# A history-attention recommender on one core: 1600 steps written out without a loop, and the head behind them reordered

## The chip, the core and the metric

One core of one Trainium2 chip runs the kernel. TensorE (PE) multiplies matrices into PSUM, VectorE (DVE) and ScalarE (ACT) work elementwise, GpSimd (POOL) issues the gathers of table rows, SyncE (SP) issues most other DMAs. The metric is the device time of one execution in microseconds (us): the median of 3 runs before the change is 32,292.97 (32,289.11 to 32,293.9).

## What is computed

The batch has 16,384 examples, each with 200 history items. With embeddings `h` (history), `it` (item), `u` (user) and `c` (category), 64 numbers each, the reference is, cut to what matters:

```python
def dice(x, alpha, axis):
    mean = jnp.mean(x, axis=axis, keepdims=True)
    var = jnp.var(x, axis=axis, keepdims=True)
    p = jax.nn.sigmoid((x - mean) * jax.lax.rsqrt(var + EPS))
    return x * (p + alpha * (1.0 - p))

h = i_emb[hist]                                  # 200 x 16384 x 64
feat = concatenate([h, itb, h - itb, h * itb])   # itb: it for every line
a = dice(feat @ au_W1 + au_b1, au_alpha, axis=1) # statistics over the batch, per history line
w = a @ au_W2 + au_b2
cur = sum(w * h, axis=0)
z = concatenate([u, it, c, cur], axis=-1)        # 256 numbers
z = dice(z @ W1 + b1, alpha1, axis=0)            # first layer, 80 numbers
z = dice(z @ W2 + b2, alpha2, axis=0)            # second layer, 40 numbers
return z @ W3 + b3                               # last layer, 2 numbers
```

All numbers are 32-bit floats. Each `dice` needs a mean and a variance over the whole batch before any of its outputs can be made.

## The kernel before

**Tiling.** The batch is cut into 8 chunks of 2,048 examples. A *step* `k` handles one chunk of one history line, so there are 200 x 8 = 1,600 steps. A chunk is gathered by 16 gathers of 128 rows each (`fetch`, L346, through `gather`, L127) into one of 16 buffers `rows`. Chunks 5 and 6 of some history lines have one of their 16 pieces fetched row by row by SP or ScalarE instead (the classes `SyncQueue` and `ScalarQueue`; `ask` in L447 hands out these fetches, the loads of their addresses and their scaling ahead of time). There are 25,350 history gathers in all.

**A step** (L421) works on several chunks at once: it fetches chunk `k`, transposes chunk `k-1` (`turn`), multiplies it with the attention weights (`product`), adds the item's part and takes statistics of chunk `k-3` (`hidden`, `measure`), and weighs and sums chunk `k-10` (`gate`, `weights`, `weigh`, where LAG is 10) into the running sums `cur`. After the last chunk of a line, `moments` turns its statistics into a scale and a shift. The order on each engine is, but for small shifts, the order in which the program is written.

**The loop.** `BODY` is 192 history lines. A loop over them (L504) has two passes of 96 lines, 768 steps each, written out inside. The other 8 lines, 64 steps, are written out behind it. In the first steps of the first pass, the chunks `k-1`, `k-3` and `k-10` do not exist yet; the same code runs on zeroed buffers then. For this, the start zeroes `hT`, `xs`, `hm` and `rows[2:]`, prepares statistics and clears PSUM.

**The start** (L465 to L501). SP loads ids, first history ids and attention weights. GpSimd gathers the 8 item chunks into `rows[0]` and `rows[1]` in turn. VectorE transposes each (`transpose`, four 64x512 instructions), SP stores it to DRAM for later reloads (`load_items`), and TensorE and ScalarE make the item's part `itp`. A gather that overwrites a buffer waits for the transposes of what was there. Behind the items come first fetches of single rows, `head_weights` (L229: VectorE zeroes the head's weight tiles, SP issues 45 small loads into them, VectorE computes `1 - alpha` and the averaging matrices `same_a` and `same_b`) and the zeroing of `rows[2:]` (L501).

**The head** (from L508). For each chunk `c`, 16 gathers fetch category rows (`j = 2c`) and 16 user rows (`j = 2c + 1`). `head_layer` multiplies four 128x1024 tiles (user, item, category, `cur`; `cur` is transposed first) with `w1a` and `w1b`: 64 of the 80 outputs of two half batches fill 128 rows of PSUM (`za`), the other 16 of each fill 32 rows, and four chunks of these are stacked to 128 rows (`zb`). Category and item are multiplied when the category rows are there, `cur` and user when the user rows are. `head_moments` (L555) gives mean and variance over the batch, with two small matmuls with `same_a` or `same_b` that average over rows. `dice` (L574) is one sigmoid on ScalarE and two VectorE operations (L577, L578). The second layer (L585 to L595) multiplies `cur` (which now holds the first 64 outputs) with `w2a`, 128 rows, and one 32-row quarter of `ab` with 32 rows of `w2b` (L592), into four PSUM tiles in turn; ScalarE evacuates (L594), VectorE takes statistics (L518). The last layer multiplies with `w3`, four chunks into one PSUM tile, and for each group of four, transposes, adds the bias and sends the outputs (L604 to L624).

Of the kernel before, what the change touches and what calls it, by code (L numbers as in the profile page):

```python
# [14 lines left out]
P = 128  # L15
# [5 lines left out]
LPB = 96  # L21
# [15 lines left out]
def din_kernel(  # L37
# [36 lines left out]
    BODY = L - L % LPB if L > LPB else 0  # L74
# [79 lines left out]
    def transpose(dst, of):  # L154
        for i in range(2):
            for e in range(2):
                nc.vector.transpose(by_tile(dst[ts(e, D)], i), of[ts(i, D), :, ts(e, S)])  # L157
# [58 lines left out]
    w2b = make("w2b", P, P)  # L216
# [4 lines left out]
    res = [make(f"res{i}", P, 4, TD, ZO) for i in range(2)]  # L221
# [7 lines left out]
    def head_weights():  # L229
# [8 lines left out]
        for g in range(2):  # L238
# [23 lines left out]
    class Queue:  # L262


        def __init__(self, engine, tiles, group, lead, span, buffers, addresses):
            self.engine, self.tiles, self.group, self.lead, self.span = engine, tiles, group, lead, span
            self.buffers, self.addresses, self.n = buffers, addresses, len(buffers)
            self.per = P // group

# [12 lines left out]
        def events(self, k, count):  # L282
            for m in range(count):
                q = m * self.per
                if self.when(q) - 8 == k:
                    yield self.load, m
                if self.when(q) - 5 == k:
                    yield self.scale, m
            for q in range(count * self.per):
                if self.when(q) == k:  # L290
                    yield self.fetch, q

        def load(self, m, l0):
            j = NC + SIDES.index(self.tiles[m % len(self.tiles)][1])
            nc.sync.dma_start(self.addresses[m % self.n], r_hist[ds(l0 + self.line(m), 1), j * P : (j + 1) * P])

        def scale(self, m, l0):
            nc.vector.tensor_scalar_mul(self.addresses[m % self.n], self.addresses[m % self.n], ROW)

        def fetch(self, q, l0):  # L300
# [120 lines left out]
    def step(k, last=None, rows_by_scalar=()):  # L421

        def has(j):
            return last is None or j <= last

        if has(k):
            fetch(k)
# [11 lines left out]
        for q, l0 in rows_by_scalar:  # L439
            by_scalar.fetch(q, l0)  # L440
# [6 lines left out]
    def ask(k, l0, n, more):  # L447
        late = []
        for q in queues:
            per = len(q.tiles)  # L450
            for what, m in q.events(k, n * per // PERIOD + (more and 2)):
                if q is by_scalar and what == q.fetch:
                    late.append((m, l0))
                else:
                    what(m, l0)
        return late

    def steps(l0, n, more):
        for k in range(n * ND):
            l, c = divmod(k, ND)  # L460
            if c == 0 and l + 1 < n + more:
                load_hist_ids((l + 1) % IDX, l0 + l + 1, by_address(l + 1))
            step(k, rows_by_scalar=ask(k, l0, n, more))

    with tc.manual_schedule():  # L465
# [6 lines left out]
        for t in (*hT, *xs, *side, *aside, *hm):  # L472
# [21 lines left out]
        for t in px:  # L494
            layer(t, [(blk_m, hm[0])])
        load_items(0)
        for k in range(-16, 0):
            ask(k, 0, L, 0)
        head_weights()
        for t in rows[2:]:  # L500
            nc.vector.memset(t, 0.0)  # L501
# [6 lines left out]
    K = (L - BODY) * ND  # L508
# [3 lines left out]
    zb = flat_rows[3:5]  # L512
    pz = [px[K % 2], px[(K + 1) % 2], pg, py]
# [141 lines left out]
```

## Time and profile before

| | us |
|---|---|
| median of 3 runs | 32,292.97 |
| the profiled execution | 32,292.57 |
| its span, first to last instruction | 32,290.8 |
| GpSimd busy | 24,281.4 (75%) |
| VectorE busy | 22,882.8 (71%) |
| TensorE busy | 9,918.7 (31%) |
| ScalarE busy | 6,057.9 (19%) |

The profile is of one execution. An instruction's row gives the source line, the engine, the operation, what it writes and reads, and how often; then the busy time, or start and duration. In brackets or behind a bar stands the idle time of the engine ahead of it and what ended that. Issuing a DMA is not busy time; a gather (`DMA_INDIRECT`) is GpSimd's own work. "PEclk" is the share of TensorE's clock that was granted. One 128x128x512 matmul in 32-bit floats shows as two matmul records.

The share of busy time is even over the run: of 40 equal slices, the first is 6 tenths for VectorE, the last 5, all others 7; GpSimd is at 7 in all but the last.

### The profile page before, as it was taken

The numbers are of one execution on the slowest core, as the hardware profiler recorded it, in microseconds if no ns is written. First come the engines' busy times: TensorE is split into PE (matmuls) and PEld (weight loads), VectorE is DVE, ScalarE is ACT, GpSimd is POOL, SyncE is SP. The second block draws the span as 40 slices with busy tenths as digits, with TensorE's granted clock in tenths as the row PEclk, the third lists the DMA queues.
The fourth block names the chain that finished last, engine by engine and source line by source line (L and its number), as shares of the span: only waits on it lengthen the run. The fifth ranks groups of instructions, "written<-read, shape, count | busy, mean of one in ns | idle before, by whom it ended". The sixth has DMA issues, their size and how long they took to land.

```text
span 32290.8 us, 175696 instructions
## 1 busy us (share of the span) xinstructions
PE 9918.7 (31%) x13212; PEld 3717.7 (12%) x13212; DVE 22882.8 (71%) x31911; ACT 6057.9 (19%) x5738; POOL 24281.4 (75%) x25739
## 2 busy tenths in 40 slices
PE   2333323333333333233233333333333333333334
PEld 1111111111111111111111111111111111111111
DVE  6777777777777777777677777777777777777775
ACT  1111111111111111111111111111111111111111
POOL 7777777777777777777777777777777777777776
PEclk6666666666666666666666666666666666666666
DMA  2222222222222222222222222222222222222221
GB/s 55 54 54 53 54 54 54 54 54 54 54 54 54 54 54 53 54 54 54 53 54 54 54 53 54 54 54 54 53 54 54 54 54 53 54 54 54 54 53 39
DMA packets 1179260, 1726.19 MB, mean 53 GB/s; under 512 B 559010, under 2 KB 559260, under 8 KB 1177980
## 3 DMA queue, kind: packets, MB, share of 16 engines
q0 software_dynamic: 823488, 844.90, 15.1%
q1 hardware_dynamic: 328604, 866.62, 7.8%
q14 instruction: 1175, 9.63, 0.1%
q10 hardware_dynamic: 25888, 3.33, 0.1%
q8 instruction: 105, 1.72, 0.0%
HBM read 1708.61 MB, written 4.33 MB: 53 GB/s over the span
## 4 chain that ended last, share of the span: by engine, by line
POOL 32%; issue 11%; DMA 4%; DVE 4%; ACT 1%; PE 0%; SPq 0%; DVEq 0%; POOLq 0%; ACTq 0%
POOL rows L128 32%; DMA rows<-in_L_rec_i_emb,idx 4%; DVE hT L157 1%; DVE xs L376 0%; DVE st L381 0%; DVE pg L359 0%; DVE py L358 0%; ACT L354 0%; DVE py L360 0%; DVE py L372 0%; ACT pg L354 0%; ACT pg L355 0%; DVE pg L364 0%; DVE other L408 0%; DVE mv L404 0%
## 5 line engine op out<-in xcount | busy, mean ns | idle before, releaser
L128 POOL DMA_INDIRECT rows<-in_L_rec_i_emb,idx x25350 | 23918.5, 944 | 7749.0 <-issue 7452.1
L162 PE MATMUL px<-hT,blk_h 128*128 128x512 f32 x6404 | 5972.1, 1088 | 21637.1 <-DVE xs L376 21622.7
L157 DVE STREAM_TRANSPOSE hT<-rows 64x512 f32<-64x512 f32 x6404 | 4518.4, 706 | 7674.6 <-DMA rows<-in_L_rec_i_emb,idx 7476.0
L391 ACT COPY py<-hT 128x1024 f32<-128x1024 f32 x1601 | 1627.3, 1016 | 24930.0 <-DVE hT L157 24930.0
L162 PEld LDWEIGHTS px<-hT,blk_h 128*128 128x128 f32 x6404 | 1880.6, 324 | 24758.2 <-DVE xs L376 23104.6
L162 PE MATMUL px<-hm,blk_m 128*128 128x512 f32 x6412 | 3970.5, 752 | 369.2 <-DVE hm L398 368.0
L358 DVE TENSOR_TENSOR py<-pg,xs 128x1024 f32<-128x1024 f32 x1610 | 1985.0, 1233 | 615.7 <-ACT pg L355 468.9
L162 PEld LDWEIGHTS px<-hm,blk_m 128*128 128x128 f32 x6412 | 1757.9, 277 | 3276.1 <-issue 1878.5
L381 DVE BATCH_NORM_STATS2 st<-xs 128x6 f32<-128x512 f32 x3206 | 2062.3, 685 | 55.1
L359 DVE STREAM_TRANSPOSE pg<-py 128x1024 f32<-128x1024 f32 x1610 | 2037.1, 1265 | 55.9
L360 DVE TENSOR_REDUCE py<-pg 128x32 f32<-128x1024 f32 x1610 | 1985.0, 1233 | 54.7
L372 DVE TENSOR_TENSOR py<-rows,pg 128x1024 f32<-128x1024 f32 x1610 | 1978.3, 1229 | 55.2
L373 DVE TENSOR_TENSOR cur<-py,cur 128x1024 f32<-128x1024 f32 x1610 | 1970.7, 1224 | 55.6
L376 DVE TENSOR_TENSOR xs<-px,itp 128x1024 f32<-128x1024 f32 x1603 | 1963.2, 1225 | 50.6
L354 ACT ACTIVATE pg<-xs,sh,rs 128x1024 f32<-128x1024 f32 x1610 | 1937.1, 1203 | 35.3 <-DVE py L372 32.6
L398 DVE TENSOR_TENSOR hm<-py,itT 128x1024 f32<-128x1024 f32 x1601 | 1933.9, 1208 | 0.0
L355 ACT ACTIVATE pg<-pg,au_al,au_1al 128x1024 f32<-128x1024 f32 x1610 | 1895.0, 1177 | 54.2
L364 DVE SCALAR_TENSOR_TENSOR pg<-py,au_bias,part 32x16 f32<-32x16 f32 x6440 | 1538.9, 239 | 227.0
L361 DVE COPY part<-py 64x32 f32<-64x32 f32 x1610 | 312.6, 194 | 55.9
L354 ACT ACT_TABLE_LOAD x204 | 261.7, 1283 | 3.6
L171 ACT ACT_TABLE_LOAD x203 | 260.4, 1283 | 7.5 <-PE pg L565 4.0
L408 DVE COPY other<-mv 32x2 f32<-32x2 f32 x804 | 158.6, 197 | 15.1
(138 smaller groups left out, 1514.0 us busy)
## 6 DMA issues: line engine op xcount, KB each, us to landing
itT<-items SPq DMA_DIRECT2D x1609, 512.0 KB
rows<-in_L_rec_i_emb,idx POOLq DMA_INDIRECT x25350
side<-in_L_rec_i_emb SPq DMA_DIRECT2D x19200, 0.2 KB
aside<-in_L_rec_i_emb ACTq DMA_DIRECT2D x12800, 0.2 KB
idx<-in_r_hist SPq DMA_DIRECT2D x200, 63.0 KB
items<-itT SPq DMA_DIRECT2D x8, 512.0 KB
idx<-in_r_hist SPq DMA_DIRECT2D x150, 0.5 KB
addr<-in_r_hist SPq DMA_DIRECT2D x150, 0.5 KB
```

Of the source, the lines that this page charges most:

```text
L128: nc.gpsimd.indirect_dma_start(out=dst[:, n, :], out_offset=None, in_=table, in_offset=bass.IndirectOffsetOnAxis(ap=ids, axis=0),)
L157: nc.vector.transpose(by_tile(dst[ts(e, D)], i), of[ts(i, D), :, ts(e, S)])
L162: nc.tensor.matmul(dst[:, ts(i, CH)], lhsT, rhs[:, ts(i, CH)], start=(first and j == 0), stop=(last and j == len(pairs) - 1), skip_group_c ...
L354: nc.scalar.activation(pg, xs[k % XR], AF.Sigmoid, bias=shifts[i], scale=rstds[i])
L358: nc.vector.tensor_mul(py, pg, xs[k % XR])
L359: nc.vector.transpose(pg, py)
L360: nc.vector.reduce_sum(total, pg.rearrange("p (n a) -> p n a", a=S), axis=mybir.AxisListType.X)
L372: nc.vector.tensor_mul(of, rows[k % ROWS], w.unsqueeze(2).to_broadcast([P, TD, D]))
L373: nc.vector.tensor_add(cur[k % ND], py, cur[k % ND])
L376: nc.vector.tensor_add(xs[k % XR], px[k % 2], itp[k % ND])
L381: nc.vector.bn_stats(stats[l % 3][:, 2 * c + i, :], xs[k % XR][:, ts(i, CH)])
L398: nc.vector.tensor_mul(hm[k % 2], py, itT[k % ITEMS])
```

## The change

The 1,600 steps are written out without a loop, `step` skips what does not exist at the start and the end, and what served the loop's first steps is gone (the zeroing of `hT`, `xs`, `hm` and `rows[2:]`, prepared statistics, cleared PSUM). `head_weights` moves ahead of the item gathers. In the head:

- `w2b` becomes four tiles of 128 rows, each zero outside one quarter, so that the second layer multiplies with 128 rows throughout.
- `cur` is transposed and multiplied with category and item, an iteration earlier than the user rows.
- The transposes of the last user chunk are split at its 12th piece.
- The two norms of the first layer share one chain; activation tables are loaded by small dummy activations (`table`).
- The first `dice` of each group of 32-row outputs comes behind the first of the 64-row outputs instead of ahead of all.
- In the last layer all eight `dice` come ahead of the transposes and outputs, and outputs alternate between SP's and ScalarE's queue. `res` lies in a row buffer that is free by then.

```diff
-LPB = 96
-    BODY = L - L % LPB if L > LPB else 0
...
-    def transpose(dst, of):
+    def transpose(dst, of, n0=0, n1=TD):
         for i in range(2):
             for e in range(2):
-                nc.vector.transpose(by_tile(dst[ts(e, D)], i), of[ts(i, D), :, ts(e, S)])
+                nc.vector.transpose(by_tile(dst[ts(e, D)], i)[:, n0:n1], of[ts(i, D), n0:n1, ts(e, S)])
...
-    w2b = make("w2b", P, P)
+    w2b = make("w2b", P, 4, P)
...
-                nc.sync.dma_start(w2b[r, g * ZA : g * ZA + Z2], W2[ZA:])
+                nc.sync.dma_start(w2b[r, j, g * ZA : g * ZA + Z2], W2[ZA:])
...
+    K = L * ND
-    def step(k, last=None, rows_by_scalar=()):
+    def step(k):
         def has(j):
-            return last is None or j <= last
+            return 0 <= j < K
+        rows_by_scalar = ask(k)
         if has(k):
+            l, c = divmod(k, ND)
+            if c == 0 and l + 1 < L:
+                load_hist_ids((l + 1) % IDX, l + 1, by_address(l + 1))
             fetch(k)
...
         attention_weights()
-        for t in (*hT, *xs, *side, *aside, *hm):
+        for t in (*side, *aside):
             nc.vector.memset(t, 0.0)
         for t in cur:
             nc.vector.memset(t, 0.0)
-        for i in range(3):
-            nc.vector.memset(rstds[i], 0.0)
-            nc.vector.memset(shifts[i], 0.0)
-        nc.vector.bn_stats(stats[-1 % 3][:, 0, :], hm[0][:, :CH])
-        for c in range(1, 2 * ND):
-            nc.vector.tensor_copy(stats[-1 % 3][:, c, :], stats[-1 % 3][:, 0, :])
+        head_weights()
...
-        for t in px:
-            layer(t, [(blk_m, hm[0])])
         load_items(0)
         for k in range(-16, 0):
-            ask(k, 0, L, 0)
-        head_weights()
-        for t in rows[2:]:
-            nc.vector.memset(t, 0.0)
-    if BODY:
-        with tc.For_i(0, BODY, LPB) as l0:
-            with tc.manual_schedule():
-                steps(l0, LPB, 1)
+            ask(k)
...
+    LATE = 12
+    def head_turn(j):
+        if j == 2 * ND - 1:
+            transpose(ucT[j % 4], spare[j % 3], 0, LATE)
+            transpose(ucT[j % 4], spare[j % 3], LATE, TD)
+        else:
+            transpose(ucT[j % 4], spare[j % 3])
     def head_layer(j):
         c, u = divmod(j, 2)
         if u == 0:
-            pairs = ((2, ucT[j % 4]), (1, itT[(K + c) % ITEMS]))
+            transpose(hT[c % TURNED], cur[c].rearrange("p (n d) -> p n d", d=D))
+            pairs = ((2, ucT[j % 4]), (1, itT[(K + c) % ITEMS]), (3, hT[c % TURNED]))
         else:
-            transpose(hT[c % TURNED], cur[c].rearrange("p (n d) -> p n d", d=D))
-            pairs = ((3, hT[c % TURNED]), (0, ucT[j % 4]))
+            pairs = ((0, ucT[j % 4]),)
...
     with tc.manual_schedule():
-        steps(BODY, L - BODY, 0)
+        for k in range(K):
+            step(k)
         for j in range(2 * ND + 2):
...
-            step(K + j, last=K - 1)
+            step(K + j)
+            if 2 <= j and j % 2 == 0:
+                head_layer(j - 2)
             if 1 <= j <= 2 * ND:
-                transpose(ucT[(j - 1) % 4], spare[(j - 1) % 3])
-            if j >= 2:
+                head_turn(j - 1)
+            if 2 <= j and j % 2 == 1:
                 head_layer(j - 2)
...
+        def table(f):
+            nc.scalar.activation(early, eps, f)
-        def head_moments(i, same):
+        def head_moments(parts):
...
+            for j, (_, same) in enumerate(parts):
+                nc.tensor.matmul(py[:, j : j + 1], same, dev[:, j : j + 1], start=True, stop=True)
+            std = small.tile([P, n], F32, tag=f"hstd{n}", name="hstd")
+            nc.scalar.activation(std, py[:, :n], AF.Sqrt, bias=eps)
+            table(AF.Sigmoid)
...
-        na, nb = head_moments(0, same_a), head_moments(1, same_b)
+        table(AF.Sqrt)
+        na, nb = head_moments([(0, same_a), (1, same_b)])
         ab = ucT[:2]
-        for j in range(2):
-            dice(ab[j], zb[j], nb, al1b, alb)
...
+        for c in range(ND):
+            dice(cur[c], za[c], na, al1a, ala)
+            if c % 4 == 0:
+                dice(ab[c // 4], zb[c // 4], nb, al1b, alb)
+            for h in range(2):
+                cols = ts(h, CH)
+                nc.tensor.matmul(pz[c % 4][:, cols], w2a, cur[c][:, cols], start=True, stop=False)
+                nc.tensor.matmul(pz[c % 4][:, cols], w2b[:, c % 4], ab[c // 4][:, cols], start=False, stop=True)
             if c:
+                second(c - 1)
+        second(ND - 1)
+        table(AF.Sqrt)
+        (n2,) = head_moments([(2, same_a)])
...
-                nc.sync.dma_start(
+                (nc.sync, nc.scalar)[q % 2].dma_start(
...
+        for c in range(ND):
+            g, q = divmod(c, 4)
+            dice(cur[c], z2[c], n2, al12, al2)
+            layer(pz[2 * g], [(w3[:, q], cur[c])], first=q == 0, last=q == 3)
+        for g in range(2):
+            answer(g)
```

`second(c)` is the evacuation and the statistics of chunk `c` as before, and `answer(g)` the transpose, the bias and the outputs of group `g`.

More of the change, by code (lines that the diff above doesn't have):

```diff
@@ L445, in step, with ask @@
             weigh(k - LAG)
[L447 removed]
+    def ask(k):
         late = []
         for q in queues:
[L450 to L451 removed]
+            for what, m in q.events(k, L * len(q.tiles) // PERIOD):
                 if q is by_scalar and what == q.fetch:
[L453 removed]
+                    late.append(m)
                 else:
[L455 removed]
+                    what(m)
         return late
[L458 to L463, printed above, removed]
     with tc.manual_schedule():
@@ L512, in din_kernel @@
     zb = flat_rows[3:5]
+    res = [
+        flat_rows[2][:, i * 4 * TD * ZO : (i + 1) * 4 * TD * ZO].rearrange("p (i n o) -> p i n o", i=4, n=TD)
+        for i in range(2)
+    ]
     pz = [px[K % 2], px[(K + 1) % 2], pg, py]
```

90 lines of the change are left out of this document (40 added, 50 removed).

## The prediction

> **What bounds the kernel now.** I read the page first (span, costliest groups), then GpSimd's waits and its timeline, then the windows and timelines of the start and of the end.
>
> ```profile
> span 32290.8 us, 175696 instructions
> L128 POOL DMA_INDIRECT rows<-in_L_rec_i_emb,idx x25350 | 23918.5, 944 | 7749.0 <-issue 7452.1
> ```
> The 25,350 gathers of the history take 23,918.5 us busy and 7,749.0 us idle ahead of them: 31,667.5, or 1.249 us each, and with 384 gathers of items, categories and users at the same pace they fill 32,147 of the 32,290.8 us. VectorE is busy 71% and waits. So GpSimd sets the pace of everything but the end, and only two kinds of time are left to win: breaks in the row of gathers, and what comes after the last one.
>
> ```profile
> POOL rows L128 <- issue: 7562.4, 24770, 11.1
> POOL rows L128 <- DVE rows L501: 7.1, 1, 7.1
> POOL rows L128 <- DMA addr<-in_r_hist: 3.2, 1, 3.2
> ```
> ```profile
> 209.72 0.94 POOL L128 DMA_INDIRECT rows<-in_L_rec_i_emb,idx  x1 [7.10 <-DVE rows L501]
> ...
> 15371.16 0.94 POOL L128 DMA_INDIRECT rows<-in_L_rec_i_emb,idx  x1 [11.07 <-issue]
> 15372.40 0.95 POOL L128 DMA_INDIRECT rows<-in_L_rec_i_emb,idx  x1 [0.30 <-issue]
> ```
> ```profile
> 3.08 1.09 POOL L128 DMA_INDIRECT rows<-in_L_rec_i_emb,ids  x1 [2.00 <-DMA ids<-in_r_item]
> ```
> The first fence is GpSimd's waits (total, times, longest), the others its timeline (start, duration, idle time before). A gather normally idles 0.30 us. Three idle longer behind the first, which starts at 3.08: 7.1 (for the zeroing of `rows`, L501), 11.1 (the loop's jump back, before 15,371) and 3.2 (the loop's exit). Above the usual 0.30 they are 6.8 + 10.8 + 2.9 = 20.5 us. There is no fourth.
>
> ```profile
> 32148.92 2.44 DMA rows<-in_L_rec_u_emb,ids
> 32151.68 2.92 DVE L157 STREAM_TRANSPOSE itp<-rows 64x512 f32<-64x512 f32 x4 [7.21 <-DMA rows<-in_L_rec_u_emb,ids]
> 32156.12 8.96 PE px L162 x16
> 32167.45 0.57 DVE L557 BATCH_NORM_AGGREGATE hmv<-zst 128x2 f32<-128x96 f32 x1
> 32170.55 0.26 DVE L557 BATCH_NORM_AGGREGATE hmv<-zst 128x2 f32<-128x24 f32 x1
> 32174.80 2.37 ACT L576 ACTIVATE hm<-rows,hshift,hrstd 128x1024 f32<-128x1024 f32 x2
> 32182.26 2.05 PE L591 MATMUL px<-cur,w2a 128*128 128x512 f32 x2 [9.52 <-DVE cur L578]
> 32246.45 1.11 ACT L594 ACTIVATE rows<-py,bias 128x1024 f32<-128x1024 f32 x1 [6.90 <-PE py L592]
> 32254.90 2.37 ACT L576 ACTIVATE hm<-rows,hshift,hrstd 128x1024 f32<-128x1024 f32 x2
> 32283.17 1.74 SPq L616 DMA_DIRECT2D out<-res  x4
> ```
> These rows (the first and the third from the chain of waits, the others from the engines' timelines) cut the end into pieces: last gather issued at 32,148.9, first norm at 32,167.5, second layer from 32,182.3 to 32,246.4, outputs issued from 32,283.2, end at 32,290.8. Some 141 us follow the last gather, and 64.2 of them are the second layer.
>
> ```profile
> 32182.30:32246.30 64.00, 64.00 (x64) 15.92 (x64) 22.40 (x28) 14.56 (x13) 0.00 (x0) 0.50 0.00 0
> 32096.20:32112.20 16.00, 16.00 (x32) 5.10 (x32) 3.14 (x5) 2.22 (x2) 12.08 (x13) 0.90 0.15 27
> ```
> These are windows (stretch, its length, busy us of TensorE, its weight loads, VectorE, ScalarE and GpSimd, granted clock, DMA). In the second layer TensorE is busy without a break, 64 matmuls in 64 us, at a granted clock of 0.50 to the last. In a stretch of the first layer, also without a break, 32 matmuls take 16 us at 0.90. What differs is L592, whose weights use 32 rows of the array; L591 and the first layer use 128.
>
> **The change, part by part.**
>
> *No loop, no zeroing of `rows`.* The three breaks go: 20.5 us. What stands on each engine inside a step is as before, so the pace of the gathers should stay.
>
> *`head_weights` moved ahead of the item gathers.* This adds a wait.
>
> ```profile
> 15.28 0.15 DVE L210 TENSOR_TENSOR au_al<-au_al,au_w 128x1 f32<-128x1 f32 x1
> 36.37 0.91 DVE L475 MEMSET cur<- 128x1024 f32 x1 [0.16 <-issue]
> 206.80 0.15 DVE L253 TENSOR_SCALAR al1b<-alb 128x1 f32<-128x1 f32 x1 [5.58 <-DMA alb<-in_L_rec_alpha]
> 208.15 0.23 DVE L258 TENSOR_SCALAR same_b<-same_b 128x128 f32<-128x128 f32 x1
> 208.54 0.91 DVE L501 MEMSET rows<- 128x1024 f32 x1 [0.16 <-issue]
> ```
> ```profile
> 13.32 0.29 SPq L207 DMA_DIRECT2D au_w<-in_L_rec_au_W  x1
> ...
> 185.70 0.34 SPq L236 DMA_DIRECT2D w1a<-in_L_rec_W  x1
> ```
> VectorE is done with the attention weights at 15.4, zeroes the small side buffers and eight `cur` (0.91 + 0.16 each) until 24.5, and `w1a`, half as long as a `cur`, until 24.9. Only then may SP issue the head's 45 loads. From the first of them to the arrival of the last `alb` takes 206.80 - 185.70 = 21.1 us, so `al1b` runs at 46.0, and behind it on VectorE stand `same_a` and `same_b` (1.6) and then the first item transposes, four of 64x512 (2.9 as in the row at 32,151.68): done at 50.5. GpSimd's 33rd gather overwrites that buffer and is due at 3.08 + 32 x 1.249 = 43.1. After L501 the step from VectorE's end (209.45) to the gather was 0.27, so it starts at 50.8 instead: 7.6 us, and nothing behind it can pass. Its bounds: 0, if the loads come early enough to be hidden, and 10, if they are slower beside the start's own traffic. I take 7.3. SP's item stores and the first reload queue behind the 45 loads too, but by then those are issued. Net for the gathers: 13.2 us.
>
> *First layer's end.* The transposes of the history's sum and the matmuls that read it move ahead, into the wait for the last user rows, and the last transposes are split so that only 64x128 pieces follow the last arrival. A 64x512 piece takes 0.73; a 64x128 is not in the trace, between 0.18 and 0.73, nearer to the small end: 0.33. Two of them precede the first matmul, which so starts at 32,152.4 on the old scale, 3.7 earlier. Then 8 matmuls follow instead of 16.
>
> ```profile
> 32258.30 9.62 PE L162 MATMUL px<-cur,w 128*128 128x512 f32 x16 [6.80 <-DVE cur L578]
> 32105.96 1.02 PE L162 MATMUL px<-itT,w1a 128*128 128x512 f32 x2
> 32106.82 1.02 PE L162 MATMUL px<-itp,w1a 128*128 128x512 f32 x2
> ```
> Sixteen from a cold start take 9.6; once the clock is up two take 0.86, so 0.43 each; in the second layer at the half clock they took 1.0 each. Eight from cold: 9.6 - 8 x 0.43 = 6.2 (bounds 3.4 and 8.0). I take 5.7, as the clock may come up earlier or later in them; the 16 of before took 9.0. Gain 3.7 + 3.3 = 7.0.
>
> *Norms.* The two first norms run as one, and the table of the sigmoid is loaded while VectorE finishes. Before, the first chain took 3.1 (to 32,170.55) and the second, with the table load, 4.25. One chain for both is the second plus the other aggregate (0.57), a second pair of small matmuls and one more small operation (together 0.4 to 1.3, taken as 1.1), less what the table load no longer waits for, two small VectorE operations (0.3): 5.6. Gain 1.7.
>
> ```profile
> L171 ACT ACT_TABLE_LOAD x203 | 260.4, 1283 | 7.5 <-PE pg L565 4.0
> 32281.49 1.25 DVE L604 STREAM_TRANSPOSE xs<-pg 128x1024 f32<-128x1024 f32 x1 [3.95 <-PE pg L162]
> ```
> For the last norm the square root's table load, 1.3, moves under the statistics, and the sigmoid's starts 0.3 earlier, less 0.1: gain 1.5. What hides it is the 1.28 of statistics on VectorE.
>
> *First `dice`.* Matmuls wait for one instead of three.
>
> ```profile
> 32214.40 1.11 ACT L594 ACTIVATE rows<-py,bias 128x1024 f32<-128x1024 f32 x1 [5.77 <-PE py L592]
> 32215.54 1.28 DVE L518 BATCH_NORM_STATS2 zst<-rows 128x6 f32<-128x512 f32 x2 [4.75 <-ACT rows L594]
> 32216.75 0.80 DVE L577 TENSOR_SCALAR rows<-rows,al1a,ala 128x1024 f32<-128x1024 f32 x1
> 32217.58 1.23 DVE L578 TENSOR_TENSOR cur<-rows,xs 128x1024 f32<-128x1024 f32 x1
> ```
> L577 and L578 take 2.0 a chunk: gain 4.0.
>
> *Second layer.* The forecast hangs on this: with 128 rows throughout I let the clock rise as in the first layer. Chunk 0 from cold: 5.7. Then a chunk needs 8 x 0.43 = 3.4 on TensorE, but its input waits on a chain: end of the chunk before last, 1.15 to the statistics (from L594 to L518), 1.2 for them, 2.0 for `dice`, and to TensorE 0.15 (between nothing and the 0.27 above): 4.5. Two chunks alternate, so two take 4.5 + 3.4 and one 4.0; seven take 28. The second `dice` of the group at chunk 4 adds 2.0 less 0.7 of slack. Sum 35.0 against 64.2: gain 29.2. TensorE then is busy 86% of the time. VectorE, 3.2 a chunk, becomes nearly as full.
>
> *Last layer.* Eight `dice` in a row take 15.9 from 1.2 after the first sigmoid's start (2.37 for two); the first 16 matmuls (from 3.4 on) end at 13.0, the rest 0.43 each at 19.9 or, with an earlier clock, 19.3; from TensorE's end to the outputs (L604 to L616) 1.7: outputs at 21.0 instead of 28.3: gain 7.2. Of the outputs the last group goes out over two queues, three deep instead of four: 0.43 each, gain 0.5. The first group's four issues no longer hide under the matmuls, but they leave under the second transpose.
>
> Sum behind the last gather: 7.0 + 1.7 + 4.0 + 29.2 + 1.5 + 7.2 + 0.5 = 51.1. With 13.2: 64.3 us. The profiled execution took 32,292.57, its span and 1.8 around it, 0.4 below the median 32,292.97. Forecast: 32,292.6 - 64.3 = **32,228 us**.
>
> The Trainium skill, "TensorE: Matmul & The Clock Gate", Part 1, says that the array's clock doubles after about 3.4 us of sustained matmul activity and names no condition on rows. The row of the second layer, 0.50 over 64 us, contradicts it as it stands. By that rule the weights' rows would not matter, and what holds the clock down there would remain: the first rival. "Runtime: NRT & Kernel Launch", Instruction fetch mechanics, says that a taken branch breaks the sequential fetch of code; the 11.07 us at the jump back agree.
>
> **The rivals.**
>
> *The clock stays down in the second layer* because its cause is something else, say the alternation of two weights. For it: the clock did not rise there once. Against: the first layer alternates weights as well and gets 0.90. Then that layer costs 64 again and 29.2 are lost: 32,257.
>
> *The new wait at the start does not come*, since the loads land sooner on a quiet queue. For: SP is idle from 13.6 on. Against: the 21.1 us are nearly all issues, one behind the other. Then 7.3 more: 32,221.
>
> *Slower: gathers in code that runs only once idle longer.* GpSimd would fetch 25,350 gathers' code without a second pass. At 0.31 instead of 0.30 idle each (a single step of the printed scale) the sum is 253 us, hence 32,482; it outweighs the gain from 2.5 ns a gather on and shows as slower from 5.1 ns on.
>
> ```profile
> 2000.00:4000.00 2000.00, 609.63 (x813) 229.77 (x811) 1428.46 (x1984) 374.54 (x356) 1511.64 (x1603) 0.63 0.23 54
> 16000.00:24000.00 8000.00, 2444.80 (x3232) 919.54 (x3232) 5710.76 (x7950) 1505.99 (x1427) 6046.03 (x6409) 0.62 0.23 54
> 31000.00:31800.00 800.00, 241.94 (x323) 91.30 (x324) 570.72 (x793) 152.41 (x145) 604.57 (x642) 0.63 0.23 53
> ```
> Against it: 1,603 gathers in 2,000 us in the loop's first pass, 6,409 in 8,000 in its second, 642 in 800 behind it, where code runs once: 1.248, 1.248 and 1.246 us.
>
> **How the numbers follow.** About 0.2%, 65 us, can be told from no change in this kernel: the bound is 32,228.4, and the forecast lies on it. The forecast's own spread is some 5 us to either side (three cold starts of 3 us each, the new wait). that is 32,223 to 32,233. I give it 0.79, and more than half of that beyond the bound, since the bounds of the new wait lie unevenly about the 7.3 taken (7.3 to gain, 2.7 to lose): 0.50 faster, 0.29 within. No wait at the start 0.10 (faster). Clock down 0.07 (within). Slower 0.04. So faster 0.60, within 0.36, slower 0.04. The range reaches from 32,215, the wait gone and warm starts besides, to 32,257, the cold second layer.
>
> **What would show it.** One wait of GpSimd of about 7 us near 43 us and no other above 1 us; the second layer at a clock of 1.00 after its first chunk, about 35 us long; 89 us from the end of the last gather to the end of the span. A second layer at 0.50, a gather pace above 1.249, or a second break at the start would make the forecast wrong.

## The result: 60.8 us faster, and the profile after

| | before | after |
|---|---|---|
| median of 18 runs each, us | 32,292.78 (32,289.11 to 32,296.22) | 32,231.94 (32,231.04 to 32,233.65) |
| profiled execution, us | 32,292.57 | 32,231.64 |
| last gather issued, us from the span's start | 32,148.92 | 32,136.62 |
| from there to the end of the span, us | 141.9 | 93.3 |

The ratio is 0.9981, with a 95% interval of 0.9974 to 0.9989. The forecast was 32,228: the kernel gained 60.8 where 64.3 were summed.

The first fence has two rows of the page after (its span; GpSimd's history gathers), the second GpSimd's waits (total, times, longest), the third its timeline (start, duration, idle time before), each of the changed kernel. Its lines are numbered two lower here than before (the gather is L126, the transposes L155).

```profile
span 32229.9 us, 174199 instructions
L126 POOL DMA_INDIRECT rows<-in_L_rec_i_emb,idx x25350 | 23918.3, 944 | 7728.6 <-issue 7468.9
```
```profile
POOL rows L126 <- issue: 7579.6, 24862, 0.3
POOL rows L126 <- DVE itT L155: 9.0, 1, 9.0
```
```profile
2.86 1.09 POOL L126 DMA_INDIRECT rows<-in_L_rec_i_emb,ids  x1 [1.78 <-DMA ids<-in_r_item]
...
41.70 0.94 POOL L126 DMA_INDIRECT rows<-in_L_rec_i_emb,ids  x1 [0.30 <-issue]
51.63 0.94 POOL L126 DMA_INDIRECT rows<-in_L_rec_i_emb,ids  x1 [8.99 <-DVE itT L155]
...
32136.62 0.94 POOL L126 DMA_INDIRECT rows<-in_L_rec_u_emb,ids  x1 [0.30 <-issue]
```
The three breaks of before are gone (the longest idle time put down to "issue" fell from 11.1 to 0.3), and one wait has come in their place, where it was expected: 9.0 before the 33rd gather, for the transposes of the item chunk whose buffer it overwrites. Idle time ahead of the history gathers fell from 7,749.0 to 7,728.6, by 20.4.

What made that wait, from the timelines of SyncE's issues and of VectorE in the changed kernel:

```profile
24.80 0.33 SPq L233 DMA_DIRECT2D w1a<-in_L_rec_W  x1
...
45.23 0.31 SPq L247 DMA_DIRECT2D alb<-in_L_rec_alpha  x1
46.76 0.15 DVE L250 TENSOR_SCALAR al1b<-alb 128x1 f32<-128x1 f32 x1 [6.47 <-DMA alb<-in_L_rec_alpha]
48.48 3.62 DVE L155 STREAM_TRANSPOSE itT<-rows 64x512 f32<-64x512 f32 x5
```
The loads start at 24.8 as predicted, the last `alb` is used 22.0 later (21.1 were taken), and the first transposes follow at 48.5. The gather was due 1.25 behind the one at 41.70, at 42.95, and started at 51.63: 8.7 lost.

The windows of the changed kernel for the gathers' pace (columns as in the prediction: the stretch, its length, busy us of TensorE, its weight loads, VectorE, ScalarE, GpSimd, granted clock, DMA share, GB/s):

```profile
2000.00:4000.00 2000.00, 613.02 (x815) 230.89 (x813) 1429.16 (x1981) 375.21 (x357) 1511.60 (x1603) 0.63 0.23 54
16000.00:24000.00 8000.00, 2441.78 (x3240) 918.66 (x3240) 5715.59 (x7958) 1508.72 (x1430) 6046.42 (x6409) 0.62 0.23 54
31000.00:31800.00 800.00, 243.44 (x320) 91.48 (x320) 568.52 (x794) 149.09 (x142) 604.60 (x642) 0.63 0.23 53
```
1,603, 6,409 and 642 gathers: the same three counts as before, to the last gather. Code that runs once was no slower here.

The end of the changed kernel, from its timeline (all engines), and its second layer from the windows:

```profile
32139.19 1.28 DVE L155 STREAM_TRANSPOSE itp<-rows 64x128 f32<-64x128 f32 x4 [2.50 <-DMA rows<-in_L_rec_u_emb,ids]
32139.87 3.78 PE L160 MATMUL px<-itp,w1a 128*128 128x512 f32 x4 [5.87 <-DVE itp L155]
32148.33 0.69 DVE L561 BATCH_NORM_AGGREGATE hmv<-zst 128x2 f32<-128x96 f32 x2
32153.54 1.23 ACT L586 ACTIVATE hm<-xs,hshift,hrstd 128x1024 f32<-128x1024 f32 x1
32157.02 2.05 PE L605 MATMUL px<-cur,w2a 128*128 128x512 f32 x2 [5.20 <-ACT rows L586]
32193.00 1.11 ACT L596 ACTIVATE rows<-py,bias 128x1024 f32<-128x1024 f32 x1 [2.93 <-PE py L606]
32199.96 2.36 ACT L586 ACTIVATE hm<-rows,hshift,hrstd 128x1024 f32<-128x1024 f32 x2
32203.35 10.13 PE L160 MATMUL px<-cur,w 128*128 128x512 f32 x16 [5.11 <-DVE cur L588]
32221.67 0.36 DVE L618 TENSOR_TENSOR rows<-xs,bias 128x64 f32<-128x64 f32 x2
```
```profile
32157.00:32193.00 36.00, 31.65 (x64) 12.12 (x64) 26.27 (x32) 15.72 (x15) 0.00 (x0) 0.94 0.00 0
32161.60:32192.90 31.30, 27.01 (x60) 10.45 (x58) 22.50 (x28) 15.69 (x14) 0.00 (x0) 1.00 0.00 0
```
The same 64 matmul records that took 64 us at a clock of 0.50 take 31.7 us of 36.0. The clock is at 1.00 from 4.6 us after the layer's start to its end. In pieces (the prediction's, from the last gather's start; the outputs' first issue is at 32,222.06, right behind the last row of the first fence):

| piece | before | after | gain | predicted |
|---|---|---|---|---|
| gathers, to the start of the last | | | 12.3 | 13.2 |
| first layer's end, to the first aggregate | 18.5 | 11.7 | 6.8 | 7.0 |
| norms, to the first sigmoid | 7.4 | 5.2 | 2.1 | 1.7 |
| first `dice`, to TensorE | 7.5 | 3.5 | 4.0 | 4.0 |
| second layer, to its last evacuation | 64.2 | 36.0 | 28.2 | 29.2 |
| last norm, to its sigmoid | 8.4 | 7.0 | 1.5 | 1.5 |
| last layer, to the last group's outputs | 28.3 | 22.1 | 6.2 | 7.2 |
| outputs, to the end | 7.6 | 7.8 | -0.2 | 0.5 |

The gains add up to the 60.9 between the two profiled executions.

### The profile page after: what moved, and what is told of

Same layout as the page of the kernel before. It is cut to its first block, busy times and chain, and to the rows that moved or that the text cites. A ratio compares the mean times of both kernels' runs of the same rounds, so it can differ in the third digit from the quotient of the medians.

```text
span 32229.9 us, 174199 instructions
## 1 busy us (share of the span) xinstructions
PE 9877.6 (31%) x13196; PEld 3707.9 (12%) x13196; DVE 22767.9 (71%) x31738; ACT 6023.5 (19%) x5711; POOL 24281.1 (75%) x25739
## 4 chain that ended last, share of the span: by engine, by line
POOL 62%; issue 22%; DMA 7%; DVE 7%; ACT 2%; SPq 0%; PE 0%; DVEq 0%; POOLq 0%; ACTq 0%
POOL rows L126 62%; DMA rows<-in_L_rec_i_emb,idx 6%; DVE hT L155 1%; DVE xs L374 1%; DVE st L379 1%; DVE py L356 1%; DVE pg L357 1%; ACT L352 1%; DVE py L358 1%; DVE py L370 1%; ACT pg L352 1%; ACT pg L353 1%; DVE pg L362 0%; DVE other L406 0%; DVE mv L402 0%
## 5 line engine op out<-in xcount | busy, mean ns | idle before, releaser
L126 POOL DMA_INDIRECT rows<-in_L_rec_i_emb,idx x25350 | 23918.3, 944 | 7728.6 <-issue 7468.9
L155 DVE STREAM_TRANSPOSE hT<-rows 64x512 f32<-64x512 f32 x6400 | 4515.7, 706 | 7794.9 <-DMA rows<-in_L_rec_i_emb,idx 7609.1
```

The lines of the kernel that those rows point to most:

```text
L126: nc.gpsimd.indirect_dma_start(out=dst[:, n, :], out_offset=None, in_=table, in_offset=bass.IndirectOffsetOnAxis(ap=ids, axis=0),)
L155: nc.vector.transpose(by_tile(dst[ts(e, D)], i)[:, n0:n1], of[ts(i, D), n0:n1, ts(e, S)])
```

## The experiments

They ran on four other chips, in four groups, and on all four the kernel before takes 38,320 to 38,411 us (medians) rather than 32,293, with single runs up to 92 us from the median. The expectations' absolute times near 32,230 were written for the first chip and missed by 5,900 to 6,130 all alike, those of the two kernels with gathers alone by 4,300. A few us can't be read from totals there, so the pieces are read from the traces, where the clock's steps and late engines move them by a microsecond or two, and the second layer's length stands out far beyond that. What is different on these chips has its own part at the end.

### How many rows the second layer's clock needs

Three kernels use fewer rows of the changed kernel's weights, each with one of the three lines for `q`; a fourth gives the kernel before nothing but the 128-row weights.

```diff
-                nc.tensor.matmul(pz[c % 4][:, cols], w2b[:, c % 4], ab[c // 4][:, cols], start=False, stop=True)
+                q = ts(c % 4, S)                       # 32 rows
+                q = ts(c % 4 // 2, 2 * S)              # 64 rows
+                q = slice(0, P if c % 4 == 3 else 3 * S)  # 96 rows
+                nc.tensor.matmul(pz[c % 4][:, cols], w2b[q, c % 4], ab[c // 4][q, cols], start=False, stop=True)
```


> The changed kernel with one edit undone: the second layer's second matmul uses 32 rows of weights again, out of the same w2b. Theory (the 32-row weights hold the clock down, as the clock is granted by the share of rows at work): granted clock 0.50 through the whole second layer, 64 us long instead of 36, time 32,260 (28 more than the changed kernel's 32,232). Rival (the clock rose for another reason, such as the new order of the first dice): second layer stays near 36 us at 1.00, time 32,232.

> The changed kernel with 64 rows of w2b in each second matmul, so that the array works with (128 + 64) / 2 = 96 rows on average, 0.75 of them. Theory (rows at work times busy share must reach about 0.8 to 0.85 of a 3.4 us window for the clock to rise): stays at 0.50, second layer 55 to 64 us, time 32,251 to 32,260. Rival (it is the alternation between a quarter and the whole array, or any use of a single quarter): clock 1.00, time 32,232.

> The changed kernel with 96 rows of w2b for three chunks of four and 128 for the fourth: 0.875 of the rows on average. Theory (a share above about 0.85 is enough): clock rises as in the changed kernel, second layer 36 to 40 us, time 32,232 to 32,236. Rival (all 128 rows are needed in every matmul): clock 0.50 at least through the first three chunks, where 96 rows are used, 10 us or more longer.

The kernel before with 128 rows (`res` moves into a row buffer, as in the change, to make room):

```diff
-    w2b = make("w2b", P, P)
+    w2b = make("w2b", P, 4, P)
...
-                nc.sync.dma_start(w2b[r, g * ZA : g * ZA + Z2], W2[ZA:])
+                nc.sync.dma_start(w2b[r, j, g * ZA : g * ZA + Z2], W2[ZA:])
...
-                    nc.tensor.matmul(pz[c % 4][:, cols], w2b[q], ab[c // 4][q, cols], start=False, stop=True)
+                    nc.tensor.matmul(pz[c % 4][:, cols], w2b[:, c % 4], ab[c // 4][:, cols], start=False, stop=True)
```


> The kernel before with 128-row w2b alone (and res in a free row buffer, and two small tiles shared, to make room). Loop, start, norms, first dice, last layer and outputs stay. Theory (the terms of the prediction add up): second layer falls from 64 to about 35 us, time 32,293 - 29 = 32,264. Rival (the gain needs the other edits of the head as well, such as the new order of dice): less than half of it, above 32,278.

Totals, median and ratio to the kernel before beside them: 38,159.8 with 32 rows (0.9958, 0.9942 to 0.9975), 38,174.6 with 64 (0.9962, 0.9949 to 0.9976), 38,175.1 with 96 (0.9960, 0.9946 to 0.9974), and 38,291.3 for the kernel before with 128 (0.9986, 0.9976 to 0.9996). The first three can't be told apart by these. The windows of the second layer can; the first fence is the kernel with 32 rows, then 64, 96, and the kernel before with 128:

```profile
38020.10:38084.30 64.20, 64.14 (x64) 15.98 (x64) 26.36 (x32) 15.72 (x15) 0.00 (x0) 0.50 0.00 0
```
```profile
38071.20:38135.40 64.20, 64.14 (x64) 15.98 (x64) 26.38 (x32) 15.73 (x15) 0.00 (x0) 0.50 0.00 0
```
```profile
38048.60:38084.90 36.30, 31.99 (x64) 12.26 (x64) 26.28 (x32) 15.73 (x15) 0.00 (x0) 0.93 0.00 1
```
```profile
38221.80:38256.10 34.30, 30.76 (x64) 12.54 (x64) 22.49 (x28) 14.56 (x13) 0.00 (x0) 0.93 0.00 1
```
Nothing differs between the first three but the rows that half of the matmuls use (in the third, every fourth chunk has all 128). With 32 and 64 (62.5% and 75% of the array's rows on the mean) TensorE is busy without a break for 64.1 us and stays at 0.50; with 96 (87.5%, in the three chunks that begin) it comes up and the layer takes 36.3, as with 128. So the cause is the number of rows at work, with the turn between 75% and 87.5% of them on the mean (64 and 96 in the smaller matmul; which of the two counts isn't told apart), and neither the alternation of two weights nor the order of the work: in the kernel before, with its own order, 128 rows alone take the layer from 64.2 to 34.3. The Trainium skill, "TensorE: Matmul & The Clock Gate", Part 1, has the clock rise after about 3.4 us of sustained activity; 64 us of sustained matmuls on 64 and 128 rows in turn did not do it, so the measurement decides against that rule as it stands.

### The wait at the start

```diff
-        head_weights()
         for c in range(ND + 1):
...
         for k in range(-16, 0):
             ask(k)
+        head_weights()
```


> The changed kernel with head_weights put back behind the item gathers (rows are still not zeroed). Theory (the wait of the 33rd gather, 8.7 us above the usual, is caused by head_weights standing ahead on VectorE, and nothing else needs them early): that wait is gone, no other of GpSimd's gathers idles over 1 us, time 32,232 - 8.7 = 32,223. Rival (the wait only moves: VectorE is late for the first history steps, and gathers wait for it there): 32,230 or more, with a new wait of GpSimd between 170 and 400 us.

38,133.9 us (0.9954, 0.9940 to 0.9967). GpSimd's waits and timeline with the weights late:

```profile
POOL rows L126 <- DMA idx<-in_r_hist: 30.4, 1, 30.4
```
```profile
43.09 0.94 POOL L126 DMA_INDIRECT rows<-in_L_rec_i_emb,ids  x1 [0.30 <-issue]
...
366.29 0.95 POOL L126 DMA_INDIRECT rows<-in_L_rec_i_emb,idx  x1 [30.41 <-DMA idx<-in_r_hist]
```
The 33rd gather, at 43.09, no longer waits. In the unedited changed kernel on these chips its wait is 23.2, since the 45 loads take longer there. So `head_weights` made the wait. But the wait moved into the stretch that the rival named, though not because VectorE is late: the loads, and 16 single rows behind them, stand in front of the ids of the second history line on SyncE's queue, and the gather that needs these waits 30.4. On these chips the move is no gain. Whether it costs anything on the first chip, where a load takes 0.4 to issue, wasn't measured.

### The cold starts

Dummy matmuls with 128 rows, into a PSUM half that is free: six ahead of the first layer's last matmuls, three and five in each norm.

```diff
+    def warm(n):
+        for _ in range(n):
+            nc.tensor.matmul(pg[:, CH:], w1a[:, 0], itp[4][:, :CH], start=True, stop=True)
```


> The changed kernel with idle TensorE time filled by 128-row matmuls whose result nobody reads, into a free PSUM bank: 6 ahead of the last first-layer matmuls, 3 and 5 in each of the two norms. Theory (three cold starts of the clock are left in the end of the changed kernel, and cost 2.6 us in the first layer, 2.6 in the second, 1.5 in the last): granted clock 1.00 at all three starts, time 32,232 - 6.5 = 32,225.5. Rival (the filling matmuls stand ahead of the norm's small matmuls and of the next layer and delay them as much as the clock gains): within 1.5 us of 32,232.

38,125.9 us (0.9949, 0.9935 to 0.9962). The timeline of TensorE with the dummies (L514), then the window of its second layer:

```profile
38042.15 5.42 PE L514 MATMUL pg<-itp,w1a 128*128 128x512 f32 x12
38047.40 1.88 PE L160 MATMUL px<-itp,w1a 128*128 128x512 f32 x4
...
38105.91 7.94 PE L160 MATMUL px<-cur,w 128*128 128x512 f32 x16 [0.71 <-DVE cur L596]
```
```profile
38061.30:38096.00 34.70, 29.53 (x65) 11.78 (x66) 26.32 (x32) 15.77 (x15) 0.00 (x0) 1.00 0.00 1
```
Mixed. The second layer starts warm and takes 34.7, where the other kernels with the changed kernel's second layer take 35.8 to 36.7, so its cold start costs 1 to 2. Ahead of the first layer's last matmuls the dummies do harm on these chips: VectorE is late, the real matmuls stand ready, and six dummies hold them up by 5.3. The last layer's 16 matmuls take 7.9 instead of 10.1 in the profile after, yet the outputs start 21.0 behind the sigmoid, no sooner than in the changed kernel where its clock came up early (next experiment): by then the eight `dice` on VectorE bound it (the last ends 17.2 behind the sigmoid in the profile after).

### The changed kernel again, and three edits at once

> The changed kernel once more, unedited, so that the next kernel has its base on the same chip. Where the single-row transfers are issued in 0.35 us each, as in the profile of the changed kernel, both theories expect 32,232 us within 3 and a ratio to the kernel before of 0.9981; where they take some 2 us each, as in the earlier experiments' chip, the theory that only the issue was slow there expects about 38,170 us and a gain larger than 61 us, since each of the two breaks removed also costs more when VectorE is behind; the rival (that the gain is a fixed 61 us wherever it is measured) expects 61 us on either chip.

```diff
-            if c % 4 == 0:
-                dice(ab[c // 4], zb[c // 4], nb, al1b, alb)
+            if c < 2:
+                dice(ab[c], zb[c], nb, al1b, alb)
```
and, as above, the dummies and `head_weights` behind the item gathers.

> The changed kernel with three more edits: the head's weights asked for behind the item gathers, dummy 128-row matmuls ahead of the head's cold layers, and the second dice for chunks 4 to 7 moved ahead by three chunks. Theory (each is a wait on the way to the end): the wait of 8.7 us before the 33rd gather goes, the two cold starts give back about 4 us each, the dice 0.7 us, so the time is about 16 us below the changed kernel's on the same chip (32,216 us where that has 32,232). Rival (the clock follows the span of recent work and the dummy matmuls only delay the real ones; the early transfer that was behind the weights was not the one waited for): within 3 us of the changed kernel.

The unedited kernel took 38,167.2 us against 38,411.2 before (0.9933, 0.9917 to 0.9950), 244 us: the rival that the gain is a fixed 61 us falls. The three edits took 38,147.0 (0.9930, 0.9914 to 0.9947), which can't be told from it. With them a gather waits 30.1 for the ids of the second line, as above. Windows of the second layer, with the three edits:

```profile
38056.20:38088.50 32.30, 28.90 (x66) 11.77 (x65) 25.65 (x31) 15.01 (x15) 0.00 (x0) 1.00 0.00 1
```
The layer takes 32.3 instead of 34.7 with dummies alone; with the same edits in the last kernel below it takes 33.0. So the second `dice` at chunk 4 costs 1.7 to 2.4 (1.3 had been put down for it). The 5 us that the dummies cost in front of the first layer take both gains back: 106.4 us from the last gather to the end without the edits, 106.6 with them.

The unedited run settles one more piece. TensorE's timeline there:

```profile
38145.47 8.63 PE L160 MATMUL px<-cur,w 128*128 128x512 f32 x16 [5.11 <-DVE cur L588]
```
The same 16 matmuls that took 10.13 in the profile after take 8.63, and the outputs start 21.0 behind the sigmoid instead of 22.1. The granted clock rose 3.1 us after the first of them here, 6.1 us in the profile after (worked out from windows of 3.4 us: a mean of 0.54 and then 1.00 here, 0.50, 0.60 and 1.00 there). Over the kernels of these four groups built on the changed one the outputs start between 21.0 and 22.1: where the clock's steps fall is chance to the code. The Trainium skill, "TensorE: Matmul & The Clock Gate", Part 1, says that the window in which activity is watched runs free of the kernel's start; these two runs of one kernel agree.

### The outputs' queues

```diff
-                (nc.sync, nc.scalar)[q % 2].dma_start(
+                nc.sync.dma_start(
...
-                    (nc.scalar, nc.sync)[q % 2].dma_start(
+                    nc.scalar.dma_start(
```


> The changed kernel with the outputs on SP alone and the two side outputs on ScalarE, as before the change. Theory of the prediction (two queues save half a microsecond of issue): 0.5 us longer from the last bias addition to the end of the span. Rival, from the trace of the changed kernel (7.8 us from the last issue's start to the end against 7.6 before): no difference or 0.3 us shorter. Total time 32,231 to 32,233 in both, so the trace decides.

38,158.0 us (0.9955, 0.9941 to 0.9969). From the last group's first issue to the end of the span it took 7.6 with all four main outputs on SyncE's queue. With the two queues it took 7.8 in the profile after, and 6.8 to 7.8 in the other kernels of these groups built on the changed one. Three or four issues deep makes no difference above this scatter.

### What the jump costs

```diff
-LPB = 96
+LPB = 48
```
In the kernel before, four passes instead of two.

> The kernel before with the loop cut finer: four passes of 48 lines instead of two of 96, so three jumps back instead of one. Theory (each jump back idles GpSimd for 10.8 us above the usual, and that is the whole price of a jump): time 32,293 + 2 x 10.8 = 32,314.5, three waits of 11 us. Rival (the wait at the jump is hidden by a shorter wait elsewhere, or is a price per run): 32,293 to 32,304.

38,440.2 us (1.0031, 1.0019 to 1.0044): 120 us more for two more jumps (73 to 169 by the interval), where the theory had 21.6. The size missed. GpSimd's timeline behind the last of its three jumps (74.5 and 82.2 behind the others):

```profile
27325.74 0.94 POOL L128 DMA_INDIRECT rows<-in_L_rec_i_emb,idx  x1 [81.44 <-issue]
```
and at the one jump of the kernel before with 128-row weights, GpSimd and VectorE:

```profile
18185.78 0.94 POOL L128 DMA_INDIRECT rows<-in_L_rec_i_emb,idx  x1 [0.30 <-issue]
18267.16 0.94 POOL L128 DMA_INDIRECT rows<-in_L_rec_i_emb,idx  x1 [80.44 <-issue]
...
18263.38 1.22 DVE L372 TENSOR_TENSOR cur<-py,cur 128x1024 f32<-128x1024 f32 x1
18266.43 2.87 DVE L157 STREAM_TRANSPOSE hT<-rows 64x512 f32<-64x512 f32 x4 [1.83 <-PEq L503]
```
VectorE at the jump of the kernel before on the first chip:

```profile
15354.82 1.22 DVE L373 TENSOR_TENSOR cur<-py,cur 128x1024 f32<-128x1024 f32 x1
15370.42 2.86 DVE L157 STREAM_TRANSPOSE hT<-rows 64x512 f32<-64x512 f32 x4 [14.38 <-PEq L504]
```
With 128-row weights GpSimd, ahead of the others, stood from 18,186.7, while VectorE worked off what it was behind until 18,264.6, and both went on at 18,266 to 18,267. So at these jumps no engine went on before all had come, and GpSimd lost its whole lead, here 78 us. On the first chip GpSimd comes last: it ended its gather at 15,360.1, VectorE its work at 15,356.0, and all went on at 15,370 to 15,371. There the 11.07 are the jump's own. Why only 1.8 follow the last engine on the other chip is open. Two losses of 74 to 82 us lie within the interval of the total. Whether a part comes back, as GpSimd, ahead of VectorE, might have waited for it later anyway, isn't shown.

### Is it the single rows that make these chips slow?

No history row is fetched singly by SyncE and ScalarE any more; GpSimd gathers all 25,600 pieces.

```diff
-BY_SP = ((1, 5), (2, 5), (3, 5))
-BY_ACT = ((1, 6), (3, 6))
+BY_SP = ()
+BY_ACT = ()
```


> The changed kernel with every history row fetched by GpSimd's gathers: SyncE and ScalarE issue no single rows, and 25,600 history gathers replace 25,350. Theory (on the experiments' chip the 32,000 single-row transfers set the pace: there each is issued 2.1 to 2.8 us after the one before where it took 0.32 before): GpSimd sets the pace on either chip, 250 more gathers at 1.2484 us each add 312 us to the changed kernel's 32,232, so 32,544 us within 5, some 15% below the kernel before on the experiments' chip and 0.8% above it on a chip where single rows are cheap; the end behind the last gather takes 93 us again and the wait before the 33rd gather 8 to 9 us again. Rival (that chip's transfers are slow of whatever kind, as by another core's traffic): within 1% of the changed kernel's 38,170 us there.

The same with the three edits of above:

> The kernel with gathers alone, and besides: the head's weights asked for behind the item gathers, dummy matmuls ahead of the head's three cold stretches, and the second dice of the group at chunk 4 moved ahead by three chunks. Theory (with GpSimd's pace even again, the end behind the last gather looks as in the changed kernel's profile, and each of these is on the path): the wait before the 33rd gather goes (8.7 us), the first layer's eight matmuls start warm (2.4), the second layer takes 32 instead of 36 us (3.8), the last layer gains 0 to 1: 15 us below the run with gathers alone, 32,529 us where that has 32,544. Rival (the dummies stand in front of the real matmuls as they did on the experiments' chip, 5 us, and the weights only come late elsewhere): 0 to 6 us below it.

36,868.0 us (0.9619, 0.9603 to 0.9635) and 36,851.8 (0.9615, 0.9598 to 0.9631). Both theories of the first fall: by the ratios it is some 3% faster than the changed kernel (1,200 us; the two ran on different chips), but it is 4,300 above what the gathers alone would take. Most of this is GpSimd's waiting for VectorE, in total 3,909.6:

```profile
POOL rows L126 <- DVE py L370: 3909.6, 266, 20.2
```
The unedited changed kernel has 5,126.3 on the same row on its chip. There VectorE also waits 3,159.1 for the reloads of items, which SyncE issues between the single rows; without these rows that wait is gone. VectorE's timeline in the kernel with gathers alone, and then in the changed kernel on the first chip:

```profile
20024.62 0.23 DVE L362 SCALAR_TENSOR_TENSOR pg<-py,au_bias,part 32x16 f32<-32x16 f32 x1 [1.21 <-issue]
20026.02 0.24 DVE L362 SCALAR_TENSOR_TENSOR pg<-py,au_bias,part 32x16 f32<-32x16 f32 x1 [1.17 <-issue]
20027.42 0.24 DVE L362 SCALAR_TENSOR_TENSOR pg<-py,au_bias,part 32x16 f32<-32x16 f32 x1 [1.16 <-issue]
```
```profile
20009.95 1.06 DVE L362 SCALAR_TENSOR_TENSOR pg<-py,au_bias,part 32x16 f32<-32x16 f32 x4
```
Four of these instructions take 1.06 on the first chip, one behind the other; here they start 1.40 apart, each after 1.2 of idle time in which it waits for nothing that the trace shows. The second kernel, 16 us below the first by the medians (15 expected), is no proof of its edits: the two ranges overlap (36,844.3 to 36,875.6 and 36,845.8 to 36,857.3). Its wait before the 33rd gather is gone, where the first has 22.2, and its second layer takes 33.0 instead of 36.6; but the dummies hold up the first layer's last matmuls by 5.3, as the rival had it, and the end behind the last gather grew from 101.1 to 108.2. Both kernels are faster than the two given ones on these chips. On the first chip 250 more gathers of 1.248 would make them some 310 us slower; that wasn't run.

## Why the prediction was right, and where its sizes were off

**GpSimd sets the pace: right.** On the first chip the gathers' counts in three stretches did not change by one, and all of the gain is breaks between gathers or time behind the last.

**The breaks and the new wait: right in place, the wait 1.4 too small.** 20.5 was forecast, and the idle time fell by 20.4. For the wait 7.3 was taken, below the 7.6 just worked out, and 8.7 measured: the loads took 0.9 more than in their old place, and the first gather started 0.2 earlier, so the 33rd was due earlier. The rival without this wait falls, and the kernel with the weights late shows that these loads made it. Here the chances leaned the wrong way: 0.60 had been put on a gain beyond 65 us, since the wait was held to have more to gain than to lose, and the gain was 60.8. The 89 us named as a sign for the stretch from the last gather's end were 92.3 (the sum itself gives 89.8).

**First layer's end, norms, first `dice`: right,** within 0.2, 0.4 and 0.0. Each 64x128 transpose took 0.32 (four in 1.28) where 0.33 was estimated between 0.18 and 0.73; eight matmuls from cold took 6.1 where 5.7 was taken.

**The second layer: the mechanism right, the size 1.0 too large.** That the rows decide is shown by the three kernels with 32, 64 and 96 rows; the clock rose as forecast. Alternation, the rival that would have left 0.50, is refuted by the kernel before with 128 rows. The terms mis-sized are chunk 0 (6.1 instead of 5.7) and, from the edits that take it out, the second `dice` at chunk 4 (1.7 to 2.4 instead of 1.3); what is left, 27.5 to 28.2, had been put at 28. The cold start as a whole costs 1 to 2.

**Last layer: 1.1 short on one draw of the clock.** The forecast's 21.0 to the outputs is what the changed kernel takes where the clock rises 3 us into the 16 matmuls, and 22.1 where it rises 6 us in, as in the profile after. A forecast from one profile can't know which.

**Outputs: wrong, by 0.7.** Three issues deep instead of four should have given 0.5. From issue to end, 7.8 against 7.6 is no gain, and the kernel with one queue took 7.6 as well. So the depth of a queue doesn't set the end; what does wasn't tried.

**Slower by code that runs once: not on the first chip,** by the equal pace. On the four other chips instructions do start late, but nearly as much in a kernel with the loop (VectorE idles 1,917.7 without a visible reason ahead of one line of the step in the kernel before with 128-row weights, 2,218.4 in the changed one), and both kernels slow down by about 6,000 us.

## What to carry to other kernels

Where TensorE shows 0.50 over a long busy stretch, look at how many rows its weights use: padding a 32-row operand with zeros to 128 rows took a stage from 64 to 36 us here, though it adds no useful work. In a kernel that one engine paces, list that engine's idle stretches above its usual gap and the time behind its last instruction; the sum of the two is all that can be won while that engine's own work and its usual gap stay, and each load moved ahead can put a wait into the list. At a jump the engines waited for the slowest one here: GpSimd idled 11 us where it came last itself, 74 to 82 where it was ahead of VectorE. So the price of a jump depends on how far ahead the pacing engine is.

## What the hardware showed that was not expected

**Instructions that start on a 0.70 us step.** On the four chips of the experiments the same code took 38,320 to 38,411 us before the change. Gathers cost what they did (944 ns of 944), VectorE's operations too, but in long stretches consecutive instructions start 0.70, 1.40 or 2.10 us apart, waiting for nothing that the trace shows, on VectorE (above) and on SyncE. Its timeline in the kernel with late weights, where the loads that start some 0.45 apart on the first chip (45 in the 20.4 between the first and the last `alb`) start 1.40 apart:

```profile
268.38 0.70 SPq L234 DMA_DIRECT2D w1b<-in_L_rec_W  x1
269.79 0.69 SPq L233 DMA_DIRECT2D w1a<-in_L_rec_W  x1
```
With the single rows taken off SyncE and ScalarE the kernel was some 3% faster there, but VectorE still lagged. What delays the instructions stays open. The Trainium skill, "Runtime: NRT & Kernel Launch", Instruction fetch mechanics, has each engine's sequencer fetch the next page of code while it executes the present one, mostly hidden; a fetch that can't keep up could look like this, but no run here shows the fetch itself.

**The gain depends on the chip.** 61 us where GpSimd paces, 244 us by the medians where other engines lag. The breaks that the change removes are longer there: in the kernel before with 128-row weights GpSimd idles 80.4 at the jump and 47.7 for the zeroing of `rows`, against 11.1 and 7.1 on the first chip. Between the profiled executions of the kernel before with 128-row weights and of the changed one on these chips, the last gather starts 115 us earlier (38,178.5 against 38,063.8), 12 us on the first chip. These are single executions on two chips, and executions there scatter by up to 92 us, so how much of the larger gain the breaks explain is open.
